# Paired lists, a float32 table A, and one base for the windows of a pair of blocks, in a graph layer on one core

## The chip, the core and the metric

The kernel runs on one core of a Trainium2 chip: TensorE (PE, its weight loads PEld), VectorE (DVE), ScalarE (ACT), GpSimd (POOL) and SyncE (SP, here only a queue that issues DMAs). The metric is the device time of one launch in microseconds. Six runs of the kernel before took 3245.58, 3245.85, 3251.91, 3271.89, 3274.26 and 3276.99 us, a median of 3261.9.

## The reference

One layer of a graph network over 12,500 nodes with 64 features and 212,500 edges sorted by `dst` (100,000 random pairs in both directions and a loop at each node, so 17 edges end at a node on average):

```python
h = jnp.maximum(_layernorm(x, axis=-1), 0.0)
edge_in = jnp.concatenate([h[src], h[dst], edge_weight1], axis=1)   # 64 + 64 + 1
e = jax.nn.silu(edge_in @ eW1 + eb1)                                # 128
e = jax.nn.silu(e @ eW2 + eb2)
agg = jax.ops.segment_sum(e, src, num_segments=N)
node_in = jnp.concatenate([h, agg], axis=1)
out = x + jax.nn.silu(node_in @ nW1 + nb1) @ nW2 + nb2
```

## The kernel before

**Tables.** The first product is split: A = h @ eW1[:64] is needed at an edge's source, B = h @ eW1[64:128] at its destination. `products` (L614) makes both for four buckets of nodes at a time, 25 times. B goes to `tb` in float32. A goes to `ta` as three bf16 parts whose sum is the float32 value: ACT rounds to the first part (L627), VectorE subtracts it (L629), ACT rounds again (L633), VectorE takes the last rest (L635).

**Blocks of edges.** The edges come in 208 blocks of 1024, a pair of them to a row of the lists, so 104 rows of 2048. `destinations` (L653) gives for each row and each quarter of 512 edges a start `lo`, the quarter's first destination but no more than a limit `lim`, and writes to `dests` how far each edge's destination lies above it. `load` (L282) reads the start with SP into a register and loads the 48 (`WL`) rows of `tb` from there on into a window, two quarters a block; `load_rows` (L270) loads a block's lists, `weights` (L297) its edge weights into two rows of `pick`. `count` (L312) turns `dests` into the one-hot `pick` (L317), and numbers the edges of each source bucket by a running sum. `send` (L353) multiplies `pick` with the window (L367), so that each edge has its B row with weight and bias terms, and scatters 1024 such rows with eight indirect DMAs of GpSimd into `q`, sorted by source bucket (L396).

**Buckets.** In parallel, 450 steps read `q` back (`fetch`, L438), 512 edges a step, with the A rows of the buckets. `s_lr` and `s_one_t` make a one-hot of an edge's source in its bucket; `s_pt` (L482) adds the transposed B rows and A times the one-hot in PSUM, three bf16 passes for a bucket (L495); then Silu, the second layer (`s_p2`, L527), Silu and the sum over sources (`s_seg`, L541) into `aggT`. 350 steps hold two tiles for each of two buckets, 100 steps one tile for each of four. `nodes` finishes four buckets at a time.

**Order.** The order on TensorE, VectorE, ACT and SP is written out by hand: the list `turn` (L559) gives the order in a step, and at each `None` in it pieces of `send_all` (L417), of the feeding generators `feed` and of the finished nodes are put in between. Loads of block s + 2 are issued at the beginning of block s, the lists one block ahead of that.

**The guard and the general way.** All this holds for inputs of a certain shape only, so the kernel has a guard. `checks` (L710) compares, for each row and quarter, the largest and the least destination with `lo`, and sets `bad`:

```python
            for i, (op, sign, limit) in enumerate(((OP.max, 1.0, WL - 0.5), (OP.min, -1.0, 0.5))):
                nc.vector.tensor_reduce(ends[:, i, :], fv, AX.X, op)
                nc.vector.tensor_tensor(ends[:, i, :], ends[:, i, :], lo, op=OP.subtract)
                nc.vector.tensor_scalar(ends[:, i, :], ends[:, i, :], sign, limit, op0=OP.mult, op1=OP.is_gt)
```

`count` marks buckets that overflow in the same way. The last row has only 1556 edges (`LAST`); its other 492 places (`PAD`) are filled with the last 492 destinations once more, with a source that no bucket has:

```python
            nc.scalar.dma_start(dstR[NP - 1 : NP, LAST:], vec(dst, E - PAD, 1, PAD))
```

At the end the flags are added up, loaded into registers, and under `tc.If(flag > 0)` (L852) `general_sums` does the sums over again in a general way, followed by the nodes: a loop `tc.For_i` of 1660 turns over 128 edges each (`tile_of`), plus one call for the last 20. A turn loads source, destination and weight of its edges with SP, gathers their A and B rows with two indirect DMAs of GpSimd, runs both layers on them, adds up edges of one source by a product with a matrix of equal sources, and adds the result into a table of sums in DRAM with a third indirect DMA that adds. Its tile pools have one buffer each. At the end of a turn all engines meet in a barrier and the semaphores are reset.

Of the kernel before, what the change touches and what calls it, by code (L numbers as in the profile page):

```python
# [28 lines left out]
F32 = mybir.dt.float32  # L29
# [10 lines left out]
L = 125  # L40
WL = 48
HB = 64
# [4 lines left out]
G = 4  # L47
# [22 lines left out]
def tile_gnn(ctx: ExitStack, tc: tile.TileContext, x, src, dst, ew, eW1, eb1, eW2, eb2, nW1, nb1, nW2, nb2, out):  # L70
# [104 lines left out]

    ta = dram.tile([P * NB, 3 * H], BF16, name="ta")
    tb = dram.tile([P * NB, H], F32, name="tb")
    dests = dram.tile([NP, 2, BLK], BF16, name="dests")
    bucks = dram.tile([NP, 2, BLK], BF16, name="bucks")
# [19 lines left out]
    locE = const.tile([P, 2 * TB, NP], F32, name="locE")  # L199
    base_i = const.tile([1, 4, NP], I32, name="base_i")  # L200
    NW = 4
    wins = [const.tile([P, 2, H], F32, name=f"win{i}") for i in range(NW)]
    for win in wins:
        nc.vector.memset(win, 0.0)
        for a in range(2):
            for i, row in enumerate((w1d, eb1b)):
                at = a * HB + WL + i
                nc.gpsimd.dma_start(win[at : at + 1, a, :], row[:1, :])

# [35 lines left out]
    NQ = 4  # L245
    ld = ctx.enter_context(tc.tile_pool(name="ld", bufs=4))
    wk = ctx.enter_context(tc.tile_pool(name="wk", bufs=2))
# [3 lines left out]
    with ExitStack() as work:  # L251
# [13 lines left out]
        carry = []  # L265
        blk = {}
        nblocks = -(-E // BLK)
        needed = [min(w for w, (_, end, _) in enumerate(LEVELS) if s < end) for s in range(nblocks)]

        def load_rows(s):  # L270

            if s < nblocks:
                p, g = s // 2, s % 2
                r, r2 = dests[p, g], bucks[p, g]
                bc = ld.tile([P, HALF], BF16, name="bc")
                of = bass.AP(tensor=r.tensor, offset=r.offset, ap=[[HALF, 2], [0, HB], [1, HALF]])
                nc.sync.dma_start(bc, of)
                bb = ld.tile([P, BLK], BF16, name="bb")
                nc.sync.dma_start(bb[:112], bass.AP(tensor=r2.tensor, offset=r2.offset, ap=[[0, 112], [1, BLK]]))
                blk[s] = [bc, bb]  # L280

        def load(s):  # L282

            if s < nblocks:
                p, g = s // 2, s % 2
                win = wins[s % NW]
                table, end = (tb0, NE * P) if s < EARLY else (tb, N)
                assert s < EARLY or len(done_b) == NB // G
                for a in range(2):
                    h = 2 * g + a  # L290
                    at = nc.sync.value_load(base_i[:, h, p : p + 1], min_val=0, max_val=end - WL)
                    nc.sync.dma_start(win[a * HB : a * HB + WL, a, :], table[bass.ds(at, WL), :])
                pick = ld.tile([P, HALF], F32, name="pick")
                blk[s] += [win, pick]
            load_rows(s + 1)

        def weights(s):  # L297

            if s < nblocks:
                pick = blk[s][3]  # L300
                e0 = s * BLK
                if e0 + BLK <= E:
                    of = bass.AP(tensor=ew.tensor, offset=ew.offset + e0, ap=[[HALF, 2], [1, HALF]])
                    nc.sync.dma_start(pick[WL::HB, :], of)
                else:
                    for a in range(2):
                        m = min(HALF, E - e0 - a * HALF)
                        if m > 0:
                            of = bass.AP(tensor=ew.tensor, offset=ew.offset + e0 + a * HALF, ap=[[m, 1], [1, m]])
                            nc.sync.dma_start(pick[a * HB + WL : a * HB + WL + 1, :m], of)  # L310

        def count(s):  # L312
# [3 lines left out]
            bc, bb, win, pick = blk[s]  # L316
            nc.vector.tensor_scalar(pick, bc, same, plus, op0=OP.is_equal, op1=OP.add)  # L317
            nc.vector.tensor_scalar(oh, bb[:NB, :], part[:NB, :], None, op0=OP.is_equal)
            yield
            weights(s)  # L320
            own = wk.tile([NB, BLK], F16, name="own")
# [116 lines left out]
        def fetch(i):  # L438
# [12 lines left out]
            for later in range(c + 1, len(LEVELS)):  # L451
                tc.declare_no_dep(ins, group=f"rows{later}", reason="these ranks were full before")
            tc.add_manual_dep(ins, last_rows[LEVELS[c][1] - 1].name, AFTER)
            tc.add_to_no_dep_group("loads", ins)
            a3 = ld2.tile([P, G, 3, H], BF16, name="a3")
            nc.sync.dma_start(
                a3.rearrange("l b s f -> l b (s f)"), ta_buckets[:, B * G : B * G + G]
            )
            batch[c, B] = [qt, a3, None]
            if c == len(LEVELS) - 1:  # L460
# [16 lines left out]
        def s_one_t(k):  # L477
            oneT = wk.tile([L, G, P], BF16, name="oneT")
            nc.vector.tensor_scalar(oneT, st[k].pop("lr")[:L], part1[:L, :], None, op0=OP.is_equal)  # L479
            st[k]["oneT"] = oneT  # L480

        def s_pt(k):  # L482

            (qt, a3, _), tiles = of(k)
            oneT = st[k].pop("oneT")
# [5 lines left out]
            for b, same in itertools.groupby(range(G), lambda t: tiles[t][1]):  # L491
                same = list(same)
                cols = slice(same[0], same[-1] + 1)
                for i in range(3):
                    nc.tensor.matmul(  # L495
                        pt[:, cols, :], a3[:L, b, i, :], oneT[:, cols, :], start=False, stop=i == 2, skip_group_check=True
                    )
            e1 = wk.tile([P, G, P], F32, name="e1")
# [115 lines left out]
        def products(b0, g, xs):  # L614
# [7 lines left out]
            nc.sync.dma_start(hd[:, b // 2 : (b + G) // 2, :], hr)  # L622
            yield
            got = fp.tile([P, G, H], F32, name="got")
            product(1, hr, mm, "mm", got)
            parts = fp.tile([P, G, 3, H], BF16, name="parts")
            nc.scalar.copy(parts[:, :, 0, :], rows_a)  # L627
            yield
            nc.vector.tensor_tensor(rows_a, rows_a, parts[:, :, 0, :], op=OP.subtract)  # L629
            nc.sync.dma_start(tb_buckets[:, b : b + G, :], got)  # L630
            done_b.append(b // G)
            yield
            nc.scalar.copy(parts[:, :, 1, :], rows_a)  # L633
            yield
            nc.vector.tensor_tensor(parts[:, :, 2, :], rows_a, parts[:, :, 1, :], op=OP.subtract)  # L635
            yield
            nc.sync.dma_start(ta_buckets[:, b : b + G, :], parts.rearrange("p b s f -> p b (s f)"))
            done_a.append(b // G)
            yield
# [13 lines left out]
        def destinations():  # L653

            nc.scalar.copy(f, dstR)
            lim = lp.tile([NP, 1], F32, name="lim")
            nc.vector.tensor_scalar(lim, part[:NP], EARLY / 2 - 0.5, float(N - NE * P), op0=OP.is_gt, op1=OP.mult)
            nc.vector.tensor_scalar(lim, lim, float(NE * P - WL), None, op0=OP.add)
            yield
            nc.vector.tensor_scalar(lo, fv[:, :, 0], lim, None, op0=OP.min)  # L660
            for g in range(2):
                nc.vector.tensor_tensor(
                    rowsS[:, g, 0, :].rearrange("p (a e) -> p a e", a=2),
                    fv[:, 2 * g : 2 * g + 2, :],
                    lo[:, 2 * g : 2 * g + 2, None].to_broadcast([NP, 2, HALF]),
                    op=OP.subtract,
                )
            nc.sync.dma_start(dests, rowsS[:, :, 0, :])
            yield
            lot = mm.tile([1, 4, NP], F32, name="lot", tag="mm")  # L670
            for g in range(4):
                nc.tensor.transpose(lot[:, g, :], lo[:, g : g + 1], ident[:NP, :NP])
            nc.scalar.copy(base_i, lot)
            yield

        def sources():
# [7 lines left out]
            yield  # L684
            nc.scalar.copy(rowsS[:, :, 1, :], sf.rearrange("p (g e) -> p g e", g=2))
            nc.sync.dma_start(bucks, rowsS[:, :, 1, :])
            yield
# [58 lines left out]
        with tc.tile_pool(name="lists", bufs=1, side="right") as lp:  # L746
# [6 lines left out]
            lo = lp.tile([NP, 4], F32, name="lo")  # L753
            rowsS = lp.tile([NP, 2, 2, BLK], BF16, name="rowsS")
            nc.vector.memset(srcR[96:NP, LAST:], N)
# [104 lines left out]
def general_sums(tc, N, E, NB, H, src, dst, ew, ta, tb, aggT, w1d, eb1b, w2, ident, ones, eb2r, part):  # L860
# [6 lines left out]
    with ExitStack() as ctx:  # L867
# [17 lines left out]
        def tile_of(at, n):  # L885
# [10 lines left out]
            for k, (idx, table) in enumerate(((si, ta[:]), (di, tb[:]))):  # L896
                got = gw.tile([P, H], F32, name="got1") if k else gw.tile([P, 3, H], BF16, name="got0")
                nc.gpsimd.indirect_dma_start(
                    out=got[:n] if k else got[:n].rearrange("p s f -> p (s f)"),
                    out_offset=None,  # L900
                    in_=table,
                    in_offset=bass.IndirectOffsetOnAxis(ap=idx[:n, :], axis=0),
                )
                if k:
                    nc.vector.tensor_tensor(pre[:n], pre[:n], got[:n], op=OP.add)
                    continue
                v = gw.tile([P, H], F32, name=f"v{k}")
                nc.vector.tensor_tensor(v[:n], got[:n, 0], got[:n, 1], op=OP.add)
                nc.vector.tensor_tensor(v[:n], v[:n], got[:n, 2], op=OP.add)
                nc.vector.tensor_tensor(pre[:n], pre[:n], v[:n], op=OP.add)  # L910
            sf = gw.tile([P, 1], F32, name="gsf")
# [75 lines left out]
```

## Time and profile before

| | us |
|---|---|
| median of six runs | 3261.9 |
| the profiled execution: time | 3256.6 |
| its span, first to last instruction | 3254.3 |
| PE / PEld busy | 2436.9 / 2123.7 |
| DVE / ACT busy | 1948.1 / 1116.8 |
| POOL busy | 1725.0 |
| mean granted TensorE clock | 0.854 of full speed |

"Busy" is the time in which an engine has an instruction under way. A group in the profile is all instructions of one line, engine and tiles: busy time in us and mean ns of one, then the engine's idle time before them and what ended most of it ("issue" where nothing in the profile did). The busy time by stage, in us:

| stage, us | PE | DVE | ACT | POOL | clock |
|---|---|---|---|---|---|
| 0 to 335 (tables made, first blocks) | 163 | 210 | 122 | 191 | 0.68 |
| 335 to 1000 | 441 | 378 | 176 | 395 | 0.76 |
| 1000 to 2900 | 1506 | 1192 | 667 | 1073 | 0.90 |
| 2900 to 3000 | 88 | 64 | 43 | 42 | 0.95 |
| 3000 to 3254 (last buckets, nodes) | 238 | 103 | 110 | 23 | 0.98 |

In this execution the branch at L852 passes over the general way, and none of its instructions runs.

### The profile page before, as it was taken

What the parts mean: (1) busy time and instruction counts of PE and PEld (TensorE: products, weight loads), DVE (VectorE), ACT (ScalarE), POOL (GpSimd) and SP (SyncE); (2) the same over time, 40 slices, a digit from 0 to 9 for tenths busy, and PEclk for the clock granted to TensorE, in tenths of its full rate; (3) what the DMA queues carried; (4) which work ended last, traced back from release to release, by engine and by line L of the source; (5) the groups of instructions that cost most, each with busy time, mean ns of one, the idle gap of its engine ahead of it and who ended that gap; (6) DMA issues with size and microseconds to landing.
All of it is one profiled execution on the core that took longest, in us unless ns stands there. A gap on an engine that the chain in (4) does not pass through costs nothing. (4 is left out here: it accounts for less than half of the span.)

```text
span 3254.3 us, 52671 instructions
## 1 busy us (share of the span) xinstructions
PE 2436.9 (75%) x18356; PEld 2123.7 (65%) x18356; DVE 1948.1 (60%) x3279; ACT 1116.8 (34%) x2460; POOL 1725.0 (53%) x1729
## 2 busy tenths in 40 slices
PE   3555566566678777878778788887788778778998
PEld 2433556455567676777677677766677667778987
DVE  6665556456566566666665666666656665666443
ACT  3433322222233333333333333333333333334443
POOL 4665555666665555565655555555555565444100
PEclk8665778677798888899988988889888988899999
DMA  4554555555556666554444445444444444555542
GB/s 116 176 154 136 180 167 177 171 175 184 180 193 203 188 198 213 177 170 157 159 148 146 153 154 160 150 151 155 140 145 156 159 158 132 169 190 181 195 153 77
DMA packets 259481, 532.52 MB, mean 164 GB/s; under 512 B 51137, under 2 KB 115315, under 8 KB 259004
## 3 DMA queue, kind: packets, MB, share of 16 engines
q1 hardware_dynamic: 184520, 361.75, 36.4%
q0 software_dynamic: 54144, 123.04, 10.6%
q10 hardware_dynamic: 20546, 44.30, 4.4%
q8 instruction: 148, 2.42, 0.3%
q14 instruction: 123, 1.01, 0.1%
HBM read 339.32 MB, written 189.55 MB: 163 GB/s over the span
## 5 line engine op out<-in xcount | busy, mean ns | idle before, releaser
L396 POOL DMA_INDIRECT q<-qs,to x1661 | 1684.0, 1014 | 1292.5 <-ACT qs L389 715.4
L499 ACT ACTIVATE e<-pt 128x512 f32<-128x512 f32 x450 | 270.9, 602 | 1318.3 <-remote 592.3
L328 DVE TENSOR_TENSOR_SCAN misc<-oh,misc 100x342 f32<-100x342 f16 (+1 forms) x617 | 575.8, 933 | 230.1 <-remote 129.2
L541 PE MATMUL seg<-one,e 128*128 128x125 f32 x3600 | 563.9, 296 | 143.2 <-issue 108.8
L527 PE MATMUL p<-w,e 128*128 128x128 f32 x3600 | 570.8, 301 | 85.9 <-issue 75.6
L541 PEld LDWEIGHTS seg<-one,e 128*128 128x128 f32 x3600 | 501.8, 209 | 168.1 <-issue 153.0
L479 DVE TENSOR_SCALAR oneT<-lr,part 125x512 bf16<-125x512 f32 x450 | 336.1, 747 | 445.1 <-remote 237.2
L527 PEld LDWEIGHTS p<-w,e 128*128 128x128 f32 x3600 | 506.8, 212 | 130.7 <-issue 107.2
L367 PE MATMUL qp<-win,pick 128*128 128x256 f32 x1664 | 510.9, 449 | 98.8 <-issue 65.6
L495 PE MATMUL pt<-oneT,a 125*128 125x256 bf16 (+1 forms) x3300 | 440.5, 273 | 92.0 <-issue 90.7
L367 PEld LDWEIGHTS qp<-win,pick 128*128 128x128 f32 x1664 | 357.9, 227 | 187.3 <-issue 128.4
L495 PEld LDWEIGHTS <-a 125*128 125x128 bf16 x3300 | 306.0, 105 | 152.6 <-issue 116.7
L552 DVE TENSOR_TENSOR aggT<-aggT,seg 128x500 f32<-128x500 f32 x250 | 167.8, 671 | 368.8 <-remote 138.3
L531 ACT ACTIVATE e<-p 128x512 f32<-128x512 f32 x450 | 271.7, 604 | 272.3 <-PE pt L495 80.9
L488 PE MATMUL pt<-ident,qt 128*128 128x128 f32 x1800 | 312.7, 299 | 59.2 <-issue 24.1
L378 ACT COPY qs<-qp 128x512 f32<-128x512 f32 x418 | 230.5, 588 | 333.6 <-remote 120.3
L334 DVE TENSOR_TENSOR own<-misc,oh 100x342 f16<-100x342 f32 (+1 forms) x623 | 320.1, 514 | 21.6
L508 DVE TENSOR_TENSOR one<-nodes,qt 128x500 f32<-128x500 f32 x450 | 301.5, 670 | 0.6 <-PE seg L541 0.5
L521 ACT COPY p<-b2f 128x512 f32<-128x512 f32 x450 | 269.7, 599 | 0.0
L488 PEld LDWEIGHTS pt<-ident,qt 128*128 128x128 f32 x1800 | 217.8, 154 | 78.4 <-issue 29.4
L474 PE MATMUL lr<-identb,qt 128*125 128x128 bf16 x1800 | 202.0, 234 | 74.6 <-issue 50.5
L474 PEld LDWEIGHTS <-qt 128*125 128x125 bf16 x1800 | 179.5, 148 | 97.3 <-issue 78.9
(122 smaller groups left out, 1095.0 us busy)
## 6 DMA issues: line engine op xcount, KB each, us to landing
a<-ta SPq DMA_DIRECT2D x275, 384.0 KB
qt<-q SPq DMA_DIRECT2D x175, 576.0 KB
bb<-bucks SPq DMA_DIRECT2D x208, 224.0 KB
qt<-q SPq DMA_DIRECT2D x100, 288.0 KB
bc<-dests SPq DMA_DIRECT2D x208, 128.0 KB
q<-qs,to POOLq DMA_INDIRECT x1661
q<-zeros ACTq DMA_DIRECT2D x20, 1080.0 KB
q<-zeros ACTq DMA_DIRECT2D x10, 1440.0 KB
```

The lines of the kernel that those rows point to most:

```text
L328: nc.vector.tensor_tensor_scan(run[:, :m], oh[:, cols], nil.to_broadcast([NB, m]), carry[-1] if carry else -1.0 - MID, op0=OP.add, op1=OP.add)
L334: nc.vector.tensor_tensor(own[:, cols], run[:, :m], oh[:, cols], op=OP.mult)
L367: nc.tensor.matmul(qps[t // 2][:, t % 2, :k], pick[:, t * P : (t + 1) * P], win[:, :k], start=True, stop=True)
L396: ins = nc.gpsimd.indirect_dma_start(out=q[:], out_offset=bass.IndirectOffsetOnAxis(ap=to[:k, j : j + 1], axis=0), in_=qs[:k, t % 2, a, :] ...
L474: nc.tensor.matmul(lr[:L, t, :], loc[:, at : at + 1].to_broadcast([P, L]), identb, start=True, stop=True)
L479: nc.vector.tensor_scalar(oneT, st[k].pop("lr")[:L], part1[:L, :], None, op0=OP.is_equal)
L488: nc.tensor.matmul(pt[:, t, :], qt[:, j, :H], ident, is_transpose=True, start=t == 0, stop=False, skip_group_check=True)
L495: nc.tensor.matmul(pt[:, cols, :], a3[:L, b, i, :], oneT[:, cols, :], start=False, stop=i == 2, skip_group_check=True)
L508: nc.vector.tensor_tensor(one.rearrange("p (b j) l -> p b j l", j=n), nodes1[:, None, None, :].to_broadcast(wide), loc[:, tiles[0][1] : ti ...
L527: nc.tensor.matmul(p2[:, t, :], e1[:, t, :], w2, start=False, stop=t == G - 1, skip_group_check=True)
L531: nc.scalar.activation(e2, p2, AF.Silu)
L541: nc.tensor.matmul(item[2][:, b, :], e2[:, t, :], one[:, t, :], start=j < G, stop=j >= G * (n - 1))
```

## The change

Four things change together.

A table in float32: `ta` holds A once, `products` stores it as it is, and `s_pt` makes one float32 product a bucket in place of three bf16 passes; the one-hot is float32 too.

Lists by pairs: `dests`, `bucks` and the edge weights of both blocks of a row come in one DMA each, and `pick` of both blocks is made by one instruction (except in the first row, whose blocks come singly, and the last).

One base for a row: only the first quarter's start is read from the list; quarter h starts 25 h above it (`STEP`), and each has a window of 58 rows (`WL`). SP loads one register for a row in place of four, and two DMAs bring the four windows. The limit of the base is set by the table's 12,800 rows (`NB * P`) in place of 12,500.

Buffers: three windows for a row in place of four for a block, two list buffers for a row in place of four for a block. The general way reads the float32 A.

```diff
-WL = 48
+WL = 58
+STEP = 25
+SPAN = 3 * STEP + WL
...
-    ta = dram.tile([P * NB, 3 * H], BF16, name="ta")
+    ta = dram.tile([P * NB, H], F32, name="ta")
...
-    NW = 4
-    wins = [const.tile([P, 2, H], F32, name=f"win{i}") for i in range(NW)]
+    NW = 3
+    wins = [const.tile([P, 2, 2, H], F32, name=f"win{i}") for i in range(NW)]
...
-    ld = ctx.enter_context(tc.tile_pool(name="ld", bufs=4))
+    ld = ctx.enter_context(tc.tile_pool(name="ld", bufs=2))
...
+                if g == 0 or p == 0:
+                    m = 1 if p == 0 else 2
+                    r, r2 = dests[p, 0, g], bucks[p, g]
+                    of = bass.AP(tensor=r.tensor, offset=r.offset, ap=[[BLK, 2], [0, HB], [1, m * HALF]])
+                    nc.sync.dma_start(bc[:, g : g + m].rearrange("p g e -> p (g e)"), of)
+                    of = bass.AP(tensor=r2.tensor, offset=r2.offset, ap=[[0, 112], [1, m * BLK]])
+                    nc.sync.dma_start(bb[:112, g : g + m].rearrange("p g e -> p (g e)"), of)
...
-                for a in range(2):
-                    h = 2 * g + a
-                    at = nc.sync.value_load(base_i[:, h, p : p + 1], min_val=0, max_val=end - WL)
-                    nc.sync.dma_start(win[a * HB : a * HB + WL, a, :], table[bass.ds(at, WL), :])
+                if g == 0:
+                    at = nc.sync.value_load(base_i[:, p : p + 1], min_val=0, max_val=end - SPAN)
+                    for a in range(2):
+                        rows = table[bass.ds(at, SPAN), :]
+                        of = [[H, WL], [2 * STEP * H, 2], [1, H]]
+                        of = bass.AP(tensor=rows.tensor, offset=rows.offset + a * STEP * H, ap=of)
+                        nc.sync.dma_start(win[a * HB : a * HB + WL, :, a, :], of)
...
+            elif g == 0:
+                two, _, picks = lists[p]
+                nc.vector.tensor_scalar(picks, two, same, plus, op0=OP.is_equal, op1=OP.add)
...
-                for i in range(3):
-                    nc.tensor.matmul(
-                        pt[:, cols, :], a3[:L, b, i, :], oneT[:, cols, :], start=False, stop=i == 2, skip_group_check=True
-                    )
+                nc.tensor.matmul(
+                    pt[:, cols, :], a[:L, b, :], oneT[:, cols, :], start=False, stop=True, skip_group_check=True
+                )
...
+            nc.sync.dma_start(ta_buckets[:, b : b + G, :], rows_a)
+            done_a.append(b // G)
...
-            nc.scalar.copy(parts[:, :, 0, :], rows_a)
-            yield
-            nc.vector.tensor_tensor(rows_a, rows_a, parts[:, :, 0, :], op=OP.subtract)
...
-            nc.scalar.copy(parts[:, :, 1, :], rows_a)
-            yield
-            nc.vector.tensor_tensor(parts[:, :, 2, :], rows_a, parts[:, :, 1, :], op=OP.subtract)
...
-            nc.vector.tensor_scalar(lim, part[:NP], EARLY / 2 - 0.5, float(N - NE * P), op0=OP.is_gt, op1=OP.mult)
-            nc.vector.tensor_scalar(lim, lim, float(NE * P - WL), None, op0=OP.add)
-            yield
-            nc.vector.tensor_scalar(lo, fv[:, :, 0], lim, None, op0=OP.min)
+            nc.vector.tensor_scalar(lim, part[:NP], EARLY / 2 - 0.5, float((NB - NE) * P), op0=OP.is_gt, op1=OP.mult)
+            nc.vector.tensor_scalar(lim, lim, float(NE * P - SPAN), None, op0=OP.add)
+            yield
+            nc.vector.tensor_scalar(lo[:, 0:1], fv[:, 0, 0:1], lim, None, op0=OP.min)
+            for h in range(1, 4):
+                nc.vector.tensor_scalar(lo[:, h : h + 1], lo[:, 0:1], float(h * STEP), None, op0=OP.add)
```

## The prediction

> **What bounds the kernel now.** I read the page first, then the stages, then the stretch after the last output.
>
> ```profile
> span 3254.3 us, 52671 instructions
> ...
> L396 POOL DMA_INDIRECT q<-qs,to x1661 | 1684.0, 1014 | 1292.5 <-ACT qs L389 715.4
> ...
> L541 PE MATMUL seg<-one,e 128*128 128x125 f32 x3600 | 563.9, 296 | 143.2 <-issue 108.8
> L527 PE MATMUL p<-w,e 128*128 128x128 f32 x3600 | 570.8, 301 | 85.9 <-issue 75.6
> ...
> L495 PE MATMUL pt<-oneT,a 125*128 125x256 bf16 (+1 forms) x3300 | 440.5, 273 | 92.0 <-issue 90.7
> ```
>
> TensorE is busy 75% of the span and no other engine above 60%; its idle time before the large groups is mostly "issue" (nothing that the profile shows). By stages it is busy 163 us of the first 335, 1506 of the 1900 from 1000 us on, and 238 of the last 254. So TensorE's order of work bounds the main path. Its timeline, columns start and length, in a steady stretch:
>
> ```profile
> 2002.61 0.82 PE L495 MATMUL pt<-oneT,a 125*128 125x256 bf16 x6
> 2003.26 1.06 PE L527 MATMUL p<-w,e 128*128 128x128 f32 x8
> 2004.16 1.05 PE L541 MATMUL seg<-one,e 128*128 128x125 f32 x8
> 2005.05 1.90 PE L367 MATMUL qp<-win,pick 128*128 128x256 f32 x8
> 2006.78 0.39 PE L474 MATMUL lr<-identb,qt 128*125 128x128 bf16 x4
> ```
>
> From start to start: six bf16 passes of 256 columns take 0.65 us, eight f32 passes of 128 take 0.90, eight f32 passes of 256 take 1.73, so 0.216 each. Every f32 product is two passes (3600 for 1800).
>
> The end of the span decides this case: the flag is worked out and loaded, and a branch jumps over the second, general way of computing everything.
>
> ```profile
> 3242.45 0.28 DVE L849 TENSOR_REDUCE m<-fp 1x1 f32<-1x128 f32 x1 [0.43 <-PE fp L847]
> 3242.77 0.14 DVE L850 CAST flag_i<-m 1x1 int32<-1x1 f32 x1
> ```
> ```profile
> L852 PEldq COMPARE_BRANCH  x1: 3355/3355/3355, 3243.5 to 3243.5; - x1
> ...
> L852 POOLq INC_SWDGE_SEM  x1: 1942/1942/1942, 3244.3 to 3244.3; - x1
> ```
> ```profile
> L983 POOLq DRAIN  x3: 50/109/7173, 3246.3 to 3254.0; - x3
> ```
>
> Columns are least, median and largest ns, then first and last start. These three show what a far jump and clearing the software DMA queue's semaphores cost.
>
> **The guard.** checks() (L710-718) sets the flag where a quarter's destinations don't all lie within WL of that quarter's start lo. Before, each quarter has its own start: its first destination, at most N-WL = 12452. After, only the first quarter does, at most 12800-133 = 12667, and quarter h starts 25 h later. The change touches neither the guard nor the filling of the last row. That row holds 1556 real edges and then, from place 1556 of 2048 on, the last 492 destinations once more (L761), so quarter 3 is 20 real edges followed by dst[212008] to dst[212499]. The reference's inputs give dst[210944] = 12406 for the row's first edge and dst[212008] = 12471. Before, quarter 3 starts at min(12499, 12452) = 12452, and 12471 is 19 above it. After, it starts at 12406 + 75 = 12481, and 12471 is 10 below: -(-10) > 0.5, so bad is 1 and the flag is 1. Every other quarter lies within 0 to 50 of its start, below 58. It isn't chance: the repeated edges reach back 1064 edges short of the row's first, at 17 edges a node 63 nodes, less than 75. So I forecast that the branch falls into general_sums.
>
> **The general way, added.** It runs after the whole main path: a loop of 1660 turns of 128 edges, one rest of 20, then 100 loads of sums and 25 node batches. Its pools have one buffer, and each turn ends in a full barrier that clears semaphores, so a turn's chain is serial. Its steps, each with my value and (low/high):
> - SP issue of si and its landing: by the trace's landing records the window loads land 2.4 us after issue in the median, 1.4 in the best tenth: 2.5 (1.5/4.0).
> - Two gathers by GpSimd in a row. Nearest row: the scatter L396, 0.97 us, one every 1.27, landing 2.1 after its start at the least and 3.5 in the median. 1.27 + 2.4: 3.7 (3.4/4.8).
> - One VectorE add: 0.2 (0.2/0.3); the other ten VectorE steps (0.15 to 0.28 us each) lie beside the gathers.
> - Transpose, Silu, f32 product, Silu, product by same, copy: three times TensorE (0.3 to 0.6; at 2000.19, slowed, eight of L541's passes take 1.5 us instead of 0.9), three times ACT at 0.27 (L378, 128 columns), seven hops of 0.04 to 0.11 as between L847, L849 and L850: 3.1 (2.4/3.6).
> - Scatter with add: 2.1 least as above; reading the target is extra and has no row: 3.0 (2.1/4.5).
> - End of turn: SP's twelve semaphore waits stand 0.062 us apart in the final sequence (0.75), a barrier there takes 0.57, twice, and the branches some 0.3: 2.3 (1.9/3.0).
> - GpSimd's clearing of three semaphores and its drain. Two rows far apart: 0.2 us at the program's start (27 + 183 ns), 9.1 at its end (1.94 + 7.17) for eight semaphores. I take three eighths of the latter, 3.4 (0.2/9.1).
>
> Sum 18.2 us (11.7/29.3), by 1660 turns and the rest 30,230 us (19,430/48,670). The 100 sums loads run one behind another, some 3.3 us each (load 2.4, transpose 0.4, copy 0.27 and hops): 330. Node batches at the 4.3 us an xr load takes: 110. Zeroing 6.5 MB at the page's mean 164 GB/s: 40. Together 480 (350/650).
>
> **Main path.** *Float32 A:* with two tiles to a block (350 steps) six bf16 passes become four f32 ones: 4 x 0.216 - 0.65 = +0.21 us; with one tile (100 steps) twelve, 0.68 us at 2960.62, become eight, 0.90: +0.22. Sum 74 + 22 = +96 us on the binding engine (+115 at the mean clock 0.85; as little as 0 where a step waits for others). oneT in f32 keeps its 747 ns, its nearest row being L508 at 670.
>
> The Trainium skill ("TensorE: Matmul & The Clock Gate", Weight-path perf modes) says that weights load fast only when they aren't FP32, which speaks against this part; the trace has a median of 98 ns for a's bf16 loads and 190 for f32 ones. By the rule alone 1100 products would pay 2 x 190 - 3 x 98 = 86 ns, 95 us more; by the row at L527, where loads of 190 ns stand 111 apart under the passes, nothing.
>
> *Products:* 25 groups lose two ACT casts (637, 626 ns) and two subtractions (693, 685), 66 us over two engines in the first 335 us, where VectorE is 63% and ACT 36% busy: -15 us (0/-34). *Lists:* picks of two blocks at once save about 6 us of VectorE; it is 60% busy, so 0. On SP a pair drops three register loads (0.42 us each), two window issues (0.27), two list issues (0.42) and a weights issue (0.5): 3.1 us; SP's own waits hold 1135 us at L447 for VectorE's one, so 0, and the longer issue of a pair delays only qt fetches that wait there. Cover gone, the saving would be 104 x 3.1 = 320 us of SP time. *Bytes:* -35 MB for A, +2 MB for windows, of 532: 0 at a DMA share near 0.5. Loads of a pair take the place of those of its first block, as far ahead as before. Main path: +80 (-60/+115).
>
> **Sum.** 3257 (the profiled execution, against a median of 3262 and runs from 3246 to 3277) + 80 + 30,230 + 480 = 34,050; I say 34,000 us.
>
> **Rivals.** *The clearing is dear:* GpSimd pays the whole 9.1 us each turn, and one engine's loop lies across an instruction block so that its branch costs TensorE's 3.36: T = 18.2 + 5.7 + 3.4 = 27.3, 49,000 us. For it: the two rows; against: they stand once, after 1661 scatters. The skill ("Runtime: NRT & Kernel Launch", Instruction fetch mechanics) says a taken branch out of the two-page window waits for its page; the row of 3355 ns agrees for a far jump, and no row has a near one. *The clearing is cheap:* the start's 0.2 us and unloaded landings: T near 13, 25,400 us.
>
> *The guard stays silent* (I misread a slice or a clamp): then the main path alone, 3,340. *The same, and faster:* between 2007.3 and 2010.2 two window issues on SP take 2.84 us while L495's passes come 0.7 apart. Such "issue" stalls hold 468 us before seven groups of TensorE's matmuls. If half the register loads and issues took a third of them, -156 + 80 gives 3,180; it decides once over 80 of the 468 go. Against: TensorE stalls alike at 2050 us, after SP's issues are done.
>
> **Numbers.** Forecast 0.62, dear 0.15, cheap 0.18, silent guard and slower 0.03, silent and faster 0.02. The range 24,000 to 45,000 leaves out the last two, most of the dear case beyond 45,000, and turns below 12.2 us, some 0.2 together. About 1% is what a measurement of this kernel tells from no change: faster 0.02, same 0.01, slower 0.97.
>
> **What would show it.** Right: a span over 20 ms; L-lines of tile_of in the costliest groups, 1660 or 1661 times each; a second indirect-DMA shape with adding; TensorE's share far below 10%. T is the span less some 3.8 ms, by 1661. On the main path: 2200 f32 passes at the pt line, no ACT cast of parts. Wrong: no instruction after the branch, and a span of 3.1 to 3.4 ms.

## The result, and the profile after

The changed kernel takes 29,358.3 us (median of 20 runs, 29,325 to 29,381) beside 3257.1 us for the kernel before (46 runs, 3224.7 to 3298.1): 9.02 times as long, 95% interval [9.007, 9.037]. The forecast of 34,000 us was 16% too long; its range of 24,000 to 45,000 holds the time.

The page of the kernel after: its span, the busy time of the engines, and four of its costliest groups (busy time, mean ns of one, then the idle time before them and what ended it).

```profile
span 29343.5 us, 232560 instructions
...
PE 8101.5 (28%) x31041; PEld 5365.6 (18%) x31041; DVE 6028.2 (21%) x21428; ACT 2503.1 (9%) x7543; POOL 7664.6 (26%) x6746
...
L945 POOL DMA_INDIRECT sums<-gadd,gti x1661 | 2696.1, 1623 | 9214.4 <-ACT gadd L944 9214.4
L910 POOL DMA_INDIRECT got<-ta,si x1661 | 1640.1, 987 | 10108.3 <-DMA di<-in_dst_dram 10103.1
...
L918 DVE CAST gsf<-si 128x1 f32<-128x1 int32 x1661 | 255.2, 154 | 17362.0 <-DMA si<-in_src_dram 17362.0
...
L910 POOL DMA_INDIRECT got<-tb,di x1661 | 1580.4, 951 | 505.7 <-DVE off L926 504.2
```

The costliest groups are lines of `tile_of`, the body of the general way, 1661 times each, which no row of before had. No engine is busy above 28%. VectorE's first step of a turn waits 17.4 ms in all for `si` to land, GpSimd 10.1 ms for `di` and 9.2 ms for ACT's last copy: most of a turn each engine waits for a landing or for another engine. Where it begins is shown by the rows of the flag (least, median and largest ns, first and last start):

```profile
L862 DVE CAST flag_i<-m x1: 141/141/141, 3175.9 to 3175.9; 1x1 int32<-1x1 f32 x1
```

The main path is over at 3175.9 us (in the profile of before the same cast starts at 3242.8); the 26,168 us behind it are the general way. The first of its 1661 scatters starts 34 us after the flag (the zeroing of the sums is in that), the last at 28,920.7, and the loads of sums and the nodes take the 423 us after it. A turn takes 25,710.6 / 1660 = 15.49 us. One of them in the timeline of the kernel after (start us, length us):

```profile
3298.24 0.33 SPq L900 DMA_DIRECT2D si<-in_src_dram  x1
...
3300.94 0.99 POOL L910 DMA_INDIRECT got<-ta,si  x1 [6.04 <-DMA di<-in_dst_dram]
...
3302.23 0.95 POOL L910 DMA_INDIRECT got<-tb,di  x1 [0.30 <-DVE off L926]
...
3304.99 0.29 DVE L916 TENSOR_TENSOR gpre<-gpre,got 128x128 f32<-128x128 f32 x1 [1.21 <-DMA got<-tb,di]
3305.34 0.18 PEld L933 LDWEIGHTS gpt<-ident,gpre 128*128 128x128 f32 x1 [4.74 <-DVE gpre L916]
...
3306.23 0.50 PEld L938 LDWEIGHTS gp<-w,ge 128*128 128x128 f32 x2 [0.71 <-ACT ge L935]
...
3307.39 0.50 PEld L942 LDWEIGHTS gps<-ge,same 128*128 128x128 f32 x2 [0.66 <-ACT ge L940]
...
3308.22 0.27 ACT L944 COPY gadd<-gps 128x128 f32<-128x128 f32 x1 [0.88 <-PE gps L942]
3308.76 1.61 POOL L945 DMA_INDIRECT sums<-gadd,gti  x1 [5.58 <-ACT gadd L944]
3313.70 0.33 SPq L900 DMA_DIRECT2D si<-in_src_dram  x1
```

Read down the starts. From SP's issue to the first gather 2.70 us, to the sum of both gathers 4.05, to the transpose 0.35, through both layers to the scatter 3.42, and from the scatter to the next turn's first issue 4.94: 15.46. In those 4.94 us the timeline shows no work. The records of the semaphore instructions fill the gap: SP's waits pass from 3312.07 on, which I take for the scatter's landing, so 3.31 us; GpSimd's record "DRAIN" begins with the scatter and ends at 3312.22; then come two barriers with the clearing between them, so 1.63 us from 3312.07 to the next issue.

### The profile page after: what moved, and what is told of

It reads as the page before. It is cut to its first block, busy times and chain, and to the rows that moved or that the text cites. A ratio compares the mean times of both kernels' runs of the same rounds, so it can differ in the third digit from the quotient of the medians.

```text
span 29343.5 us, 232560 instructions
## 1 busy us (share of the span) xinstructions
PE 8101.5 (28%) x31041; PEld 5365.6 (18%) x31041; DVE 6028.2 (21%) x21428; ACT 2503.1 (9%) x7543; POOL 7664.6 (26%) x6746
## 5 line engine op out<-in xcount | busy, mean ns | idle before, releaser
L945 POOL DMA_INDIRECT sums<-gadd,gti x1661 | 2696.1, 1623 | 9214.4 <-ACT gadd L944 9214.4
L910 POOL DMA_INDIRECT got<-ta,si x1661 | 1640.1, 987 | 10108.3 <-DMA di<-in_dst_dram 10103.1
L937 PE MATMUL gp<-b2r,ones 1*128 1x128 f32 x3322 | 1264.2, 482 | 9346.9 <-PEq L953 9339.4
L937 PEld LDWEIGHTS gp<-b2r,ones 1*128 1x128 f32 x3322 | 823.2, 306 | 9787.7 <-PEq L953 9779.8
L910 POOL DMA_INDIRECT got<-tb,di x1661 | 1580.4, 951 | 505.7 <-DVE off L926 504.2
L916 DVE TENSOR_TENSOR gpre<-gpre,got 128x128 f32<-128x128 f32 x3322 | 970.9, 292 | 3403.1 <-DMA got<-tb,di 1960.5
L938 PE MATMUL gp<-w,ge 128*128 128x128 f32 x3322 | 1324.3, 502 | 690.8 <-ACT ge L935 690.8
L942 PE MATMUL gps<-ge,same 128*128 128x128 f32 x3322 | 1318.1, 501 | 609.2 <-ACT ge L940 609.2
L920 PE MATMUL srow<-ident,gsf 128*128 128x128 f32 x1661 | 788.4, 475 | 2281.3 <-DVE gsf L918 2281.3
L938 PEld LDWEIGHTS gp<-w,ge 128*128 128x128 f32 x3322 | 835.2, 313 | 1178.3 <-ACT ge L935 1178.3
L942 PEld LDWEIGHTS gps<-ge,same 128*128 128x128 f32 x3322 | 828.5, 309 | 1098.3 <-ACT ge L940 1098.3
L906 DVE TENSOR_SCALAR gpre<-w1d,w 128x128 f32<-128x128 f32 x1661 | 841.5, 507 | 0.0
L920 PEld LDWEIGHTS srow<-ident,gsf 128*128 128x128 f32 x1661 | 302.3, 182 | 2769.4 <-DVE gsf L918 2769.4
```

The costliest lines, as they stand in the source:

```text
L906: nc.vector.tensor_scalar(pre[:n], w1d[:n], w[:n], None, op0=OP.mult)
L910: nc.gpsimd.indirect_dma_start(out=got[:n], out_offset=None, in_=table, in_offset=bass.IndirectOffsetOnAxis(ap=idx[:n, :], axis=0),)
L920: nc.tensor.transpose(srow[:n, :n], sf[:n].to_broadcast([n, n]), ident[:n, :n])
L937: nc.tensor.matmul(p2[:n], ones[:, :n], eb2r, start=True, stop=False)
L938: nc.tensor.matmul(p2[:n], e1[:, :n], w2, start=False, stop=True)
L942: nc.tensor.matmul(ps[:n], same[:n, :n], e2[:n], start=True, stop=True)
```

## The experiments

Three questions: is it the guard; what is a turn made of; and what are the change's own edits worth once the guard is quiet, since the forecast's +80 us can't be read from the time of a kernel that runs 26 ms longer. Twelve kernels ran in three batches: e1 to e4 on a chip where the kernel before takes 3179.0 us (35 runs), e6, e8, e9 and b0, and then e7 and e10 to e12, on another (the quick chip below), where it takes 2554.7 (7 runs) and 2556.2 (13 runs). Each ratio is to the kernel before on the same chip. For the main path two theories stand against each other at first. M1 is the forecast's: TensorE binds, and float32 A lengthens its passes. M2: float32 A gains, since TensorE gets fewer instructions and loses less time before them.

### Is it the guard?

**e1_fill** changes only what fills the last row's 492 spare places: the last 123 destinations four times, in place of the last 492 once, so that a quarter never reaches back below its window.

```diff
-                nc.scalar.dma_start(dstR[NP - 1 : NP, LAST:], vec(dst, E - PAD, 1, PAD))
+                last = bass.AP(tensor=dst.tensor, offset=dst.offset + E - PAD // 4, ap=[[PAD, 1], [0, 4], [1, PAD // 4]])
+                nc.scalar.dma_start(dstR[NP - 1 : NP, LAST:].rearrange("p (c e) -> p c e", c=4), last)
```

> The changed kernel, with the 492 spare places of the last row filled with the last 123 destinations four times over in place of the last 492 once. Theory (the repeated destinations alone trip the guard): the least of them, dst[212377], lies above the quarter's start of 12481, the flag is 0, the branch passes over the general way, and the time is what the changed kernel's main path takes, its flag at 3176 us plus some 12 us of ending as before: 3190 us, 0.98 of the kernel before. Rival (another quarter or a bucket's overflow trips it as well): 29,350 us as it was.

Measured: 3168.6 us, ratio 0.9961 [0.9929, 0.9994]. The page of e1_fill:

```profile
span 3153.0 us, 48057 instructions
...
PE 2436.8 (77%) x17253; PEld 2152.6 (68%) x17253; DVE 1888.0 (60%) x3129; ACT 1098.7 (35%) x2410; POOL 1732.1 (55%) x1737
...
L513 PE MATMUL pt<-oneT,a 125*128 125x256 f32 (+1 forms) x2200 | 524.1, 368 | 24.2 <-issue 21.0
```

No instruction of the general way is left, and the whole 26 ms is gone. The fill of places that hold no edge was the cause; the 58 rows and the four starts were wide enough for every real edge. The expected 0.98 set a flag at 3176 us against 3257 us of other runs; beside the kernel before on its own chip e1_fill comes to 0.996.

**e6_forced_general** is the kernel of before with the flag's start value set to 1, so that its own general way (A in three parts, two more VectorE sums) runs behind the old main path.

```diff
-    nc.vector.memset(bad, 0.0)
+    nc.vector.memset(bad, 1.0)
```

> The kernel of before with the flag's start value set to one, so that the general way runs whatever the destinations are, after the whole main path. Its gather of A fetches three bf16 parts (768 bytes a row, against 512 after the change) and two more VectorE additions join them, some 0.2 us each, partly beside the second gather. Theory 1 (the general way costs 15.5 us a turn whatever kernel it stands in, and the rest is as after): 3257 + 26100 + 1660 x (0.2 to 0.5) = 29,700 to 30,200 us. Theory 2 (the change itself made the turn dear, by its float32 A or its windows): a turn under 13 us, below 25,500 us.

Measured in one run: 28,549.4 us, of which the main path is about 2550 on that chip, so 26.0 ms of general way, as after the change. Its scatters are 15.38 us apart in the median, those of after 15.48. So the change made no turn dear; it only let the turns run. Theory 1 had 29,700 us at the least, with a main path of 3257 us. Some 700 us of the miss are this chip's shorter main path; most of the rest are the two sums, which cost nothing, where 0.2 to 0.5 us a turn were expected: they lie where VectorE waits for the second gather. One turn of e6:

```profile
2610.14 0.29 DVE L908 TENSOR_TENSOR v<-got 128x128 f32<-128x128 bf16 x1 [0.98 <-DMA got<-ta,si]
2610.47 0.29 DVE L909 TENSOR_TENSOR v<-v,got 128x128 f32<-128x128 f32 x1
2610.79 0.29 DVE L910 TENSOR_TENSOR gpre<-gpre,v 128x128 f32<-128x128 f32 x1
2611.46 0.29 DVE L905 TENSOR_TENSOR gpre<-gpre,got 128x128 f32<-128x128 f32 x1 [0.38 <-DMA got<-tb,di]
```

### What is a turn made of?

**e7_two_tiles** puts two tiles of 128 edges into a turn of the changed kernel's loop.

```diff
-        with tc.For_i(0, ET * P, P) as at:
+        with tc.For_i(0, ET * P, 2 * P) as at:
             tile_of(at, P)
+            tile_of(at + P, P)
```

> The changed kernel with its general way, two tiles of 128 edges to a turn of its loop (830 turns instead of 1660). Theory 1, the turn's 15.5 us are a serial chain of landings and a barrier: the second tile's loads (2.7 us to the first gather) lie under the first tile's chain, and one scatter's landing and one end of turn (5.0 us together) fall away, so that a turn of two costs 15.5 + 7.8 to 10.0 = 23.3 to 25.5 us and the whole 3200 + 830 x that + 500 = 23,000 to 24,900 us. Theory 2, the cost is each tile's own (gathers, passes, scatter one behind another): two tiles cost 28 to 31 us, the whole 27,000 to 29,400 us.

Measured in one run: 20,458.9 us, below both. Some 600 us of the miss are this chip's shorter main path; the rest is the turn: from the first scatter at 2577.9 us to the last at 20,029.3 there are 830 turns of 21.0 us, and theory 1 had 23.3 at the least. The timeline of e7 in the second half of one turn:

```profile
3001.05 0.18 PEld L933 LDWEIGHTS gpt<-ident,gpre 128*128 128x128 f32 x1 [4.94 <-DVE gpre L916]
...
3001.94 0.80 PE L938 MATMUL gp<-w,ge 128*128 128x128 f32 x2
3001.96 0.94 POOL L910 DMA_INDIRECT got<-ta,si  x1 [3.18 <-DVE gto L928]
...
3003.26 0.98 POOL L910 DMA_INDIRECT got<-tb,di  x1 [0.36 <-issue]
...
3004.55 1.62 POOL L945 DMA_INDIRECT sums<-gadd,gti  x1 [0.30 <-ACT gadd L944]
...
3009.66 1.59 POOL L945 DMA_INDIRECT sums<-gadd,gti  x1 [3.49 <-ACT gadd L944]
3014.76 0.33 SPq L900 DMA_DIRECT2D si<-in_src_dram  x1
```

The second tile's first gather starts with the first tile's second layer (L938), and its scatter follows 5.1 us after the first. Theory 1 hid the second tile's loads, one landing and one end of turn, but not the gathers. The second tile adds 21.0 - 15.5 = 5.5 us, so some 10 of the 15.5 us were waits and end of turn that a second tile shares or covers.

### What are the edits themselves worth?

**e4_a_alone** is the kernel of before with float32 A and nothing else (the core; `products` stores A as it is):

```diff
-                for i in range(3):
-                    nc.tensor.matmul(
-                        pt[:, cols, :], a3[:L, b, i, :], oneT[:, cols, :], start=False, stop=i == 2, skip_group_check=True
-                    )
+                nc.tensor.matmul(
+                    pt[:, cols, :], a[:L, b, :], oneT[:, cols, :], start=False, stop=True, skip_group_check=True
+                )
```

> The kernel before with float32 A alone (table, one-hot, one pass a bucket, no rounding steps). M1: slower than the kernel before by 60 to 115 us, as the prediction has it. M2: faster by 50 to 80 us.

Measured: 3173.0 us, ratio 0.9968 [0.9931, 1.0004]: neither M1's loss of 60 us or more nor M2's gain of 50 or more.

**e2_bf16_a** is e1_fill with the opposite of that diff: A in three bf16 parts again, all other edits kept.

> e1_fill with A as three bf16 parts again (table, one-hot, three passes a bucket, the four rounding steps in products); lists by pairs and one base stay. Theory M1 (the main path's gain comes from SP's fewer register loads and issues, and float32 A costs the 96 us of TensorE that its passes add): faster than e1_fill by 60 to 100 us, near 3100. Rival M2 (float32 A is itself the gain, by a third fewer passes, fewer bytes and shorter products, and the rest does nothing): as the kernel before, 3240 to 3270.

Measured: 3167.6 us, ratio 0.9965 [0.993, 1.0], the same as e1_fill, so again neither M1 nor M2.

**e3_own_starts** is e1_fill with a start for each quarter again: 48 rows, four registers, four window loads for a row.

```diff
-                    at = nc.sync.value_load(base_i[:, p : p + 1], min_val=0, max_val=end - SPAN)
...
+                    for h in range(4):
+                        at = nc.sync.value_load(base_i[:, h, p : p + 1], min_val=0, max_val=end - WL)
```

> e1_fill with a start of its own for each quarter again: windows of 48 rows, four register loads and four window DMAs a row; lists, picks and weights by pairs and float32 A stay. M1: the gain goes back, 50 to 100 us slower than e1_fill. M2: within 20 us of e1_fill.

Measured: 3184.0 us, ratio 1.0006 [0.9974, 1.0038]: some 15 us above e1_fill, with intervals that overlap. That is within M2's 20 us and below M1's 50.

So neither the 96 us that float32 A should cost nor a gain of that size from fewer instructions showed. Two theories were left for float32 A: TensorE's supply of instructions pays 1100 pairs fewer against longer passes, or TensorE has room. The next three were meant for this; **b0_same_chip** is the kernel of before, for a profile on their chip.

> The kernel of before, unchanged, for a profile from the same chip as the next two. Both theories: pt group of 3300 bf16 passes busy about 440 us with some 90 us of 'issue' before it, TensorE's clock about 0.90 from 1000 to 2800 us, time within 1% of the kernel before beside it.

Measured: 2561.8 us, within 1% of the kernel before beside it, but both 20% below what the first chip showed; the pt group is at 385 us, not 440, and the "issue" before it is gone. The expectation had both as on the first chip. The page of b0:

```profile
span 2559.5 us, 52671 instructions
...
PE 2117.2 (83%) x18356; PEld 1950.8 (76%) x18356; DVE 1937.0 (76%) x3279; ACT 1137.6 (44%) x2460; POOL 1760.1 (69%) x1729
...
L527 PE MATMUL p<-w,e 128*128 128x128 f32 x3600 | 501.7, 284 | 7.8 <-ACT p L521 7.8
...
L495 PE MATMUL pt<-oneT,a 125*128 125x256 bf16 (+1 forms) x3300 | 384.6, 260 | 0.0
```

The same 52,671 instructions; but before the passes of L527 nothing waits for "issue" any more (75.6 us before), nor before L495 (90.7). Here TensorE is 83% busy, and the room for a longer product is smaller.

**e8_a_twice** adds a float32 product with a tile of zeros to each of e4's:

```diff
+                for w, last in ((nought[:L, :], False), (a[:L, b, :], True)):
...
-                    pt[:, cols, :], a[:L, b, :], oneT[:, cols, :], start=False, stop=True, skip_group_check=True
+                        pt[:, cols, :], w, oneT[:, cols, :], start=False, stop=last, skip_group_check=True
```

> The kernel of before with float32 A alone, and each product by A done a second time with a tile of zeros (2200 more float32 passes; what is computed stays the same). By the price of the prediction, 1400 x 0.216 + 800 x 0.1125 us = 392 us more on TensorE. Theory S, the product's passes set the time: before + 392 + 96 = ratio 1.15 (1.12 to 1.18). Theory P, each pair of weight load and product also takes a place of about 0.087 us in TensorE's supply of instructions, which is why 1100 pairs fewer paid for 96 us of longer streaming: before + 392 + 2200 x 0.087 = +583, ratio 1.18 (1.15 to 1.21). Theory N, TensorE has slack and something else sets the end: ratio below 1.04.

Measured: 2762.2 us, ratio 1.0804 [1.0786, 1.0822], between the theories. TensorE's busy time in the page grew by 405 us, from 2117.2 to 2522.5, the time by 208. By windows (length, then busy time of PE, PEld, DVE, ACT and POOL, clock, DMA share, GB/s), first b0, then e8:

```profile
1000.00:2300.00 1300.00, 1188.08 (x10733) 1119.32 (x10732) 1081.04 (x1826) 631.21 (x1333) 992.47 (x960) 0.97 0.68 212
```
```profile
1000.00:2300.00 1300.00, 1298.99 (x10107) 1218.34 (x10107) 995.26 (x1663) 574.80 (x1215) 926.26 (x888) 1.00 0.57 177
```

TensorE's idle time there, 112 us, is used up to 1. About half of the added work went into room, the rest into the time; the granted clock rose too, from 0.97 to 1.00. Where TensorE has no room a pass costs its full price: the stretch after the last scatter, further below, shows it.

**e9_small_pairs** adds three pairs of a bf16 weight load of zeros and a one-column product to each bucket of before.

```diff
+                    nc.tensor.matmul(
+                        pt[:, same[0], :1], nought[:L, :], oneT[:, same[0], :1], start=False, stop=False, skip_group_check=True
+                    )
```

> The kernel of before with 3300 more pairs of a bf16 weight load (zeros) and a product of one column, three for each bucket; what is computed stays the same. Theory S (streaming sets the time): a one-column product streams next to nothing and its load of some 25 ns lies under the passes: +0 to +82 us, ratio 1.000 to 1.026. Theory P (each pair takes about 0.087 us of supply): +290 us, ratio 1.09 (1.06 to 1.12), with 'issue' before the pt group grown by some hundred us. Theory N: ratio 1.00 to 1.01.

Measured: 2570.6 us, ratio 1.0051 [1.0035, 1.0068], so 16 us for 3300 pairs, 5 ns each on average. The loads took 95 ns each in the trace (L497, least and median) and not some 25, but nearly all of it lay under other work. A supply that costs 87 ns a pair is out on this chip. On a chip with the stalls it wasn't tried.

The last three set the edits side by side on the quick chip.

> The kernel of before with float32 A alone. Slack theory: 0.985 to 1.005 of before. Streaming theory: 1.03 on a chip without the stalls. If the pairs of lists and the one base matter for themselves, e10_fill_again lies below this one, by up to 15 us for the base (what e3_own_starts showed).

> The changed kernel with its spare places filled so that the general way stays out, as in e1_fill, on whichever chip comes. Slack theory (TensorE's 96 us more of streaming lie where it waits for scatters or stands still): ratio 0.985 to 1.005 on any chip. Streaming theory (TensorE's passes set the time wherever the stalls are few): on a chip without the stalls, where TensorE is 83% busy, +96 - 15 us, ratio 1.03; on a chip with them 0.995 to 1.005.

> The same with A as three bf16 parts, all other edits kept. Slack theory: within 1% of e10_fill_again. Streaming theory: 3% (1 to 4) faster than e10_fill_again on a chip without the stalls, the same on a chip with them.

| kernel | us | ratio to before |
|---|---|---|
| e12, float32 A alone | 2550.4 | 0.998 [0.9967, 0.9993] |
| e10, all edits, guard quiet | 2572.5 | 1.006 [1.0043, 1.0077] |
| e11, all edits but float32 A | 2593.1 | 1.0147 [1.0127, 1.0167] |

Float32 A is no net cost even here: alone it gains 6 us, between e11 and e10 20 us. The streaming theory, which had e12 at 1.03 and e10 3% behind e11, is out; e10 lies just above the slack theory's 1.005, and above e12 where it was expected up to 15 us below. The rest of the change, which cost nothing on the first chip, costs 22 us (e10 over e12) to 37 us (e11 over before) here. Rows of e12 (line 367 there) and e10 (line 388), the same product of `pick` with the window:

```profile
L367 PE MATMUL qp<-win,pick 128*128 128x256 f32 x1664 | 460.2, 426 | 61.0 <-DMA pick<-in_edge_weight_dram 30.3
```
```profile
L388 PE MATMUL qp<-win,pick 128*128 128x256 f32 x1664 | 465.8, 430 | 135.1 <-DMA pick<-in_edge_weight_dram 88.8
```

TensorE waits 74 us more before these, most of it for the edge weights, which now come for both blocks in one DMA of 8 KB. This fits the loss, and the last scatter starts 28 us later in e10 than in e12; but no run undid that one load here, nor the windows or the list buffers. Which of them it is stays open.

## Why the prediction was right, point by point

**The guard** was right, with its place: the last row's repeated edges. e1_fill shows it by removing them alone.

**The turn** was predicted at 18.2 us and took 15.49. Against the turn in the timeline:

| term | predicted (low/high) | measured |
|---|---|---|
| si issued and landed, to the first gather | 2.5 (1.5/4.0) | 2.70 |
| two gathers | 3.7 (3.4/4.8) | 4.05 |
| one sum | 0.2 | 0.35 |
| TensorE and ACT chain | 3.1 (2.4/3.6) | 3.42 |
| scatter that adds, landed | 3.0 (2.1/4.5) | 3.31 |
| end of turn; clearing and drain | 2.3 + 3.4 (2.1/12.1) | 1.63 |

Five terms were 0.15 to 0.35 us short, together 1.33 us, and so made up for a third of the sixth's error: that part of the agreement is luck. The mis-sized term is "GpSimd's clearing of three semaphores and its drain". I took three eighths of what eight semaphores cost at the program's end, 1.94 and 7.17 us. In the turn the clearing instruction takes 0.217 us in the trace and the drain after it 0.047, together 0.26 and not 3.4; the rest of the end took 1.37 us of the 2.3. GpSimd's drains and clearings at the loop's line (least, median, largest ns):

```profile
L953 POOLq DRAIN  x3318: 47/1714/9685, 3210.1 to 28896.1; - x196
...
L953 POOLq INC_SWDGE_SEM  x1659: 217/217/243, 3220.0 to 28895.9; - x185
```

Half of the drains are short. The other half, ahead of the first barrier, run beside the scatter and take 3.48 us in the median, about as long as it is under way, so the loop's drain has no one price: it goes with what precedes it. What the 7.17 us at the program's end waits for is not shown: in before the last scatter started 241 us ahead of it, and it takes the same 7173 ns in b0, e8 and e12. But no clearing in the loop costs anything like it, and the row from the program's start (0.2 us) was the right one. Scaled by 1660 the turn's 2.7 us make 4500 of the 4700 us between the sum of 34,050 and the span.

One sign that the prediction named failed: TensorE's share was to lie far below 10%, and it is 28% of the span and 21% within the loop. A turn keeps TensorE busy 3.3 us. The three steps that stand in the chain take 0.47, 0.80 and 0.79 us, where 0.3 to 0.6 were expected, and the passes of L920 and L937 lie beside the chain. The other signs held.

**Around the turns**, 480 us were predicted and 34 + 423 = 457 measured.

**The main path** was predicted at +80 us. It failed in the words "+96 us on the binding engine". The 96 us are right as busy time: from b0 to e12 the group of A's products goes from 384.6 to 480.6 us. But TensorE has next to no idle time only at the end of the main path, after GpSimd's last scatter. In this stretch it is busy 98% of the time in b0 and 99% in e12 (columns as in the windows above):

```profile
2311.00:2548.00 237.00, 233.17 (x2037) 211.26 (x2035) 100.30 (x165) 107.05 (x212) 19.93 (x27) 1.00 0.44 149
```
```profile
2285.00:2533.00 248.00, 244.72 (x1931) 221.11 (x1929) 100.42 (x166) 107.71 (x213) 21.23 (x27) 1.00 0.40 129
```

And there the time goes with A's products, whatever the chip:

| kernel | A | last scatter starts, us | from there to the cast of the flag, us |
|---|---|---|---|
| before | bf16 | 3004.8 | 237.9 |
| b0, quick chip | bf16 | 2311.8 | 236.2 |
| e9, quick chip | bf16, and small pairs | 2311.6 | 246.1 |
| e4, first chip | float32 | 2911.6 | 248.0 |
| e12, quick chip | float32 | 2285.7 | 247.1 |
| e8, quick chip | float32, done twice | 2456.3 | 294.6 |

In b0 and e12 53 of the 450 steps are left at that point. Float32 A costs 11 us in them, which is what the prediction's own prices give (11.4). The 226 further passes of e8 cost 47.5 us, by the prices 46, and the 336 small pairs of e9 10 us, 30 ns each. Ahead of the last scatter TensorE stands idle 427 of 2311 us in b0 and 353 of 2285 in e12. There e8's further passes, which come with nothing else, add 299 us of busy time to e12's and put the last scatter 171 us later, so little over half of the work reaches the time. Float32 A comes with less rounding and smaller loads, and with these together the last scatter starts earlier, not later; what its passes alone would cost there no run separates. So the price of a pass was right, and the step that failed is that all 96 us were charged to the time: 11 us show at the end, and what the rest may cost ahead of the last scatter is outweighed. That TensorE is the busiest engine was taken to mean that it is late everywhere.

Six other profiles of the main path agree: 237 and 238 us with bf16 (e11, e2), 247 to 249 with float32 (e10, e1, after, e3). On the first chip, too, float32 A was no loss in time (e4, e2), but no run there used up the idle time ahead of the last scatter, as e8 did on the quick one.

In the profiles of before and after the flag is cast at 3242.8 and 3175.9 us, so in them the changed main path is 67 us shorter, not 80 longer. They are one execution each, runs of the kernel before lie up to 73 us apart, and e1 and e10 beside the kernel before give 0.996 and 1.006: how much of the 67 us belongs to the change stays open.

**The products' -15 us** has the right sign. Rows of b0 and e12, the stores of B and the scatters:

```profile
L630 SPq DMA_DIRECT2D tb<-got x25: 337/368/562, 72.8 to 275.0; - x25
...
L396 POOL DMA_INDIRECT q<-qs,to x1661: 891/971/1861, 61.5 to 2311.8; - x185
```
```profile
L626 SPq DMA_DIRECT2D tb<-got x25: 338/368/480, 73.2 to 194.2; - x25
...
L396 POOL DMA_INDIRECT q<-qs,to x1661: 887/967/1849, 61.9 to 2285.7; - x185
```

Without the rounding the last table rows are stored 81 us earlier, and the last scatter starts 26 us earlier. From e11 to e10, which differ in the same way, it is 24 us (2338.0 and 2314.1). Whether the rounding does this or the smaller loads of A (256 KB in place of 384), no run separates. From the last scatter to the end of the span it takes 258.6 us in place of 247.7, the 11 us above, and 26 less 11 is the 15 us by which e12's span is shorter than b0's. That it equals the forecast's 15 is chance: the medians of e12 and the kernel before beside it are 6 us apart.

**Lists and bytes at nothing** held on the first chip and not on the second, by 22 to 37 us.

**The weight-load rule** of the Trainium skill ("TensorE: Matmul & The Clock Gate", Weight-path perf modes) says that weights in FP32 don't load fast. The trace agrees with the rule: the median load takes 98 ns for A in bf16 (b0, L495) and 190 ns in float32 (e10, L513). The 95 us that the prediction worked out for it as a rival price did not come: TensorE's idle time before A's float32 products is 0.0 us in e10 and e12, and the ratios of e4 and e12 leave no room for such a cost.

**The rivals.** The dear clearing fell (0.26 us). The cheap one, T near 13, had the clearing right but the landings too short. The silent guard, and the silent guard that is faster, fell with the flag. Of what they said of the main path, 3,340 us is out by e1 and e10, and the 3,180 (0.976 of the kernel before) is not borne out beside the kernel before: 0.996 and 1.006. The one profile of after does come near it, with its flag at 3175.9 us and some 12 us of ending, but that alone doesn't show the rival's reason, fewer issues on SP; e3_own_starts, which puts SP's register loads and window issues back, was 15 us slower than e1_fill, within the intervals.

## What to carry to other kernels

When a kernel guards a fast way, follow the padding through the guard as you do the data: 492 places that hold no edge cost 26 ms. Don't scale a wait that stands once, at the program's end, into a turn of a loop, and price a turn by its landings as well as by its engines. And ask of the busiest engine where it is late, stage by stage, before charging an instruction to the time: here a pass cost its full price after the last scatter and little over half of it before.

No version beats the kernel before by much: e1_fill does by 0.4% on the first chip and loses 0.6% on the second, and float32 A alone, the only one that was not slower on either, comes out 0.3% lower on the first, not clear of no change, and 0.2% lower on the second.

## What the runs showed of the hardware that was not expected

**Chips differ by a fifth on the same program.** The kernel before takes 3257 us beside the result (that chip is not on record), 3179 us on the chip of e1 to e4 and 2555 us on the quick one, there alike in both batches. The mean granted clock is 0.854 in the profile of before and 0.927 in that of b0, but VectorE's largest group is as long (L328: 575.8 and 575.2 us). What goes is mostly standing still: starts of TensorE's passes more than 0.45 us apart are 925 with 1073 us in all before, 244 with 485 us in b0, 588 of the 695 us of difference. Of the 925, 361 are 0.64 to 0.78 or 1.35 to 1.45 us long, in b0 14. About half of the 361 begin in the 2 us after GpSimd starts the last scatter of a block, where blocks are 14 us apart, and in these VectorE and ACT start few instructions as well (34 and 8; spread evenly it would be 126 and 95). The general way is as fast on either (15.48 and 15.38 us a turn), so the difference belongs to the main path. Its cause was not found. An edit worth less than a few per cent can have another sign on another chip, as the whole change with its guard quiet had (e1 and e10).

**TensorE's granted clock is low where it works little.** In the general way (windows of after):

```profile
3400.00:28900.00 25500.00, 5435.76 (x13174) 3064.66 (x13173) 4090.99 (x18111) 1348.62 (x4940) 5865.61 (x4940) 0.50 0.09 13
```

TensorE is 21% busy, and the granted clock is 0.50. The transpose at L920 takes 203 ns at the least and 475 in the median. Two tiles a turn keep TensorE 31% busy, and the clock stays at 0.50 (windows of e7):

```profile
3400.00:19900.00 16500.00, 5058.19 (x12560) 2922.00 (x12560) 3753.81 (x17269) 1287.43 (x4710) 5567.43 (x4710) 0.50 0.14 19
```
